# Four head chunks instead of five, an earlier start on TensorE, and equal shares of M's small reads

## The chip, the cores and the metric

The kernel runs on 1 core of one Trainium2 chip. The metric is the device time of one execution in microseconds (us), as the median of several runs. The span in a profile is from the first to the last instruction and lies 1.7 to 2.0 us below that time (in two runs 2.6 and 2.8). All runs quoted are of the state "fast". Ratios are the mean time of one kernel's fast runs over that of the other's fast runs of the same rounds, so not quite the ratio of the medians quoted beside them.

## The reference, cut to what matters

A three-layer cross network on x (1024 x 64 x 16, f32). For every layer: all products x[b,f,e] * h[b,g,e], then a contraction of the 64 x 64 (f, g) pairs with a weight matrix.

```python
x0 = h = x
for i in range(3):
    z = jnp.einsum('bfe,bge->bfge', x0, h).reshape(B, f0 * fh, e)
    y = jnp.einsum('oc,bce->boe', Ws[i], z) + bs[i][None, :, None]
    x_i, h = (y[:, :half], y[:, half:]) if i < 2 else (y, y)
    xs.append(x_i)
return jnp.sum(jnp.concatenate(xs, axis=1), axis=2) @ fc_w.T + fc_b
```

The last layer is only summed, so the kernel folds W2 and the final weights into W1 beforehand: the result is a matrix M, made on the chip. M has to be written to memory and read back with a skew and transposed, to become half of the weights `w_all`.

## The kernel before: what the change and the argument touch

The batch is cut into 32 chunks of 32 samples (512 columns). For each chunk VectorE makes four product tiles z (`product`), TensorE contracts them with `w_all`. Weights of the first layer (columns 0 to 63 of `w_all`) are there early; columns 64 to 127 need M. So a few "head" chunks are run with the first half alone while M is made and moved, and their second half later. Two of them, `KEPT`, keep their z tiles; the others' products are made again.

```python
HEAD = [4, 5, 6, 0, 1]; KEPT = HEAD[-2:]; FIRST = 8   # chunks from FIRST on run in groups of four
# (cut) head: chunks c0, c1; m_sb = M from w1s and v2t on TensorE; M written to md (HBM)
head(c2)                                      # products, first half, keep_h1 (ACT)
for half in range(2):                         # two large reads of M
    (nc.sync, nc.scalar)[half].dma_start(out=ms[halves[half], 0]..., in_=skewed(...))
for i in range(NI):                           # eight small reads, 256-byte rows
    for half in range(2):
        queue = nc.scalar if half and i < 2 else nc.sync
        queue.dma_start(out=ms[halves[half], 1]..., in_=skewed(...))
# (cut) dg and w_sq are read from md too
head(c3)
new_acc(c4, H2)                               # the fifth head chunk covers M's way
for j in range(NJ - 1):
    product(c4, j); half_contract(c4, 0, j)
nc.vector.tensor_tensor(w_all[:, 0:NT, 64:128], ms[:, 0], ms[:, 1], ALU.add)   # M is there
# (cut)
load_chunk(2); w1x = ...; nc.sync.dma_start(out=w1x, in_=wx1)
# (cut) second half of the kept chunks; then the main loop over chunks 2 to 31:
for s, c in enumerate(order):
    ahead = order[s + 2]                      # VectorE works two chunks ahead
    load_chunk(ahead); last_tile(ahead); [product(ahead, j) for j in range(NJ)]
    # contract c; per pair of chunks a tile y = bd x (PSUM, 2 buffers), combined on VectorE by x_v0x
```

`nc.sync` is the SP queue and `nc.scalar` the ACT queue. In the traces an engine's instructions and the DMAs that it gives out come in program order: after the change ACT gives out its five reads of M from 43.67 us on, and the square that the program puts behind them starts at 51.23.

## Time and profile before

| | before |
|---|---|
| time, median (6 runs) | 501.0 us (500.82 to 501.46) |
| span of the profile | 499.2 us |
| TensorE busy / VectorE busy | 483.8 us (97%) / 381.8 us (76%) |
| first matmul | 8.44 us |
| M added (start of that VectorE row) | 51.81 us |
| TensorE idle while M is on its way (from 40.5 us on) | none |

TensorE's row is the one to read: it is full from 40.5 us to the end of the last chunk, so a change gains by removing matmuls or by starting that full stretch sooner, and loses by opening a gap in it. The lines behind this stand in the prediction.

### The profile page before, as it was taken

What the parts mean: (1) busy time and instruction counts of PE and PEld (TensorE: products, weight loads), DVE (VectorE), ACT (ScalarE), POOL (GpSimd) and SP (SyncE); (2) the same over time, 40 slices, a digit from 0 to 9 for tenths busy, and PEclk for the clock granted to TensorE, in tenths of its full rate; (3) what the DMA queues carried; (4) which work ended last, traced back from release to release, by engine and by line L of the source; (5) the groups of instructions that cost most, each with busy time, mean ns of one, the idle gap of its engine ahead of it and who ended that gap; (6) DMA issues with size and microseconds to landing.
All of it is one profiled execution on the core that took longest, in us unless ns stands there. A gap on an engine that the chain in (4) does not pass through costs nothing.

```text
span 499.2 us, 4338 instructions
## 1 busy us (share of the span) xinstructions
PE 483.8 (97%) x1814; PEld 222.6 (45%) x1814; DVE 381.8 (76%) x233; ACT 92.5 (19%) x159; POOL 1.4 (0%) x14
## 2 busy tenths in 40 slices
PE   3899999999999999999999999999999999999996
PEld 1455654456444344443444434443444434444432
DVE  4999699988999889898777686776877777770302
ACT  1243033122111121312011121111111121010001
POOL 1000000000000000000000000000000000000000
PEclk9999999999999999999999999999999999999999
DMA  8997895353454443446144442333444430000000
GB/s 327 425 419 226 338 421 208 116 230 129 181 235 175 170 174 162 177 175 256 66 169 169 168 168 113 118 136 138 168 169 168 167 131 39 0 0 0 2 0 0
DMA packets 14787, 82.80 MB, mean 166 GB/s; under 512 B 3788, under 2 KB 4460, under 8 KB 5232
## 3 DMA queue, kind: packets, MB, share of 16 engines
q1 hardware_dynamic: 13644, 81.24, 41.5%
q10 hardware_dynamic: 1124, 1.29, 0.9%
q8 instruction: 14, 0.23, 0.2%
q14 instruction: 5, 0.04, 0.0%
HBM read 80.88 MB, written 1.64 MB: 165 GB/s over the span
## 4 chain that ended last, share of the span: by engine, by line
PE 91%; DMA 5%; ACT 1%; ACTq 0%; SPq 0%; DVE 0%; issue 0%
PE acc L198 75%; PE acc L237 11%; DMA w1s<-in_w1h 4%; PE acc L219 2%; DMA xb<-in_xrb 1%; PE acc L211 1%; PE y L267 1%; PE acc L205 1%; PE pm L336 0%; PE po L489 0%; ACT zl L175 0%; ACT zl L181 0%; ACT m_sb L341 0%; ACT xx L190 0%; ACTq L360 0%
## 5 line engine op out<-in xcount | busy, mean ns | idle before, releaser
L198 PE MATMUL acc<-z,w_all 128*128 128x512 f32 x864 | 374.1, 593 | 0.0
L166 DVE TENSOR_TENSOR z<-xa,xb 128x2048 f32<-128x2048 f32 (+1 forms) x141 | 314.9, 2270 | 49.9 <-PE acc L198 39.7
L198 PEld LDWEIGHTS acc<-z,w_all 128*128 128x128 f32 x864 | 163.3, 190 | 208.3 <-issue 207.8
L237 PE MATMUL acc<-z,w_all 128*64 128x256 f32 x640 | 74.7, 389 | 10.4 <-DVE w_all L282 8.4
L171 ACT ACTIVATE z<-xa 32x512 f32<-32x512 f32 x35 | 21.9, 625 | 323.5 <-DVE z L166 320.7
L263 DVE SCALAR_TENSOR_TENSOR uu<-acc,vs,q 64x512 f32<-64x512 f32 x27 | 20.2, 750 | 62.4 <-ACT q L262 62.3
L237 PEld LDWEIGHTS acc<-z,w_all 128*64 128x64 f32 x640 | 45.8, 140 | 39.1 <-DVE w_all L282 9.9
L274 DVE TENSOR_REDUCE acc<-uu 128x64 f32<-128x1024 f32 (+2 forms) x18 | 20.2, 1125 | 0.3
L190 ACT COPY xx<-xa 64x512 f32<-64x512 f32 x32 | 19.6, 613 | 0.4
L262 ACT COPY q<-acc 64x512 f32<-64x512 f32 x27 | 15.7, 580 | 19.3 <-PE y L224 12.9
L186 ACT ACTIVATE sq<-xa 32x512 f32<-32x512 f32 x24 | 15.1, 628 | 0.6
L270 DVE SCALAR_TENSOR_TENSOR uu<-y,cx,xx 128x512 f32<-128x512 f32 x16 | 11.4, 745 | 0.3
L224 PE MATMUL y<-xx,bd 64*64 64x512 f32 x48 | 11.6, 602 | 0.0
L219 PE MATMUL acc<-xx,v1w 64*64 64x512 f32 x48 | 11.6, 602 | 0.0
L211 PE MATMUL acc<-sq,w_sq 32*128 32x512 f32 x48 | 6.8, 640 | 0.0
L175 ACT ACTIVATE zl<-xa 64x512 f32<-64x512 f32 x11 | 6.8, 623 | 0.1
L219 PEld LDWEIGHTS acc<-xx,v1w 64*64 64x64 f32 x48 | 2.8, 132 | 7.9 <-issue 7.9
L237 PE MATMUL acc<-zl,w_all 64*64 64x256 f32 (+1 forms) x40 | 6.1, 393 | 0.0
L243 ACT ACTIVATE hb<-acc,vs 128x256 f32<-128x256 f32 x5 | 2.4, 474 | 20.0 <-PE acc L237 20.0
L495 ACT ACTIVATE res<-po,cst 2x480 f32<-2x480 f32 (+1 forms) x2 | 0.9, 464 | 24.0 <-PE po L489 24.0
L181 ACT COPY zl<-xa 64x512 f32<-64x512 f32 x8 | 4.9, 616 | 0.1
L256 DVE TENSOR_TENSOR uu<-acc,hb 64x256 f32<-64x256 f32 x10 | 4.2, 421 | 0.2
(52 smaller groups left out, 52.0 us busy)
## 6 DMA issues: line engine op xcount, KB each, us to landing
xa<-in_xra SPq DMA_DIRECT2D x34, 1024.0 KB, 4.8
xb<-in_xrb SPq DMA_DIRECT2D x34, 1024.0 KB, 7.0
w<-in_w2t SPq DMA_DIRECT2D x2, 1024.0 KB, 13.5
xa<-in_xra SPq DMA_DIRECT2D x2, 512.0 KB, 4.1
w1s<-in_w1h SPq DMA_DIRECT2D x1, 1024.0 KB, 20.3
w1x<-in_wx SPq DMA_DIRECT2D x1, 1024.0 KB, 8.7
w0x<-in_wx SPq DMA_DIRECT2D x1, 1024.0 KB, 10.3
xb<-in_xrb SPq DMA_DIRECT2D x1, 768.0 KB, 7.0
```

Of the source, the lines that this page charges most:

```text
L166: nc.vector.tensor_tensor(zs[c, j][:, i : i + n, :], xas[c][:, i : i + n, :], xbs[c][j].unsqueeze(1).to_broadcast([128, n, N]), ALU.mult,)
L171: nc.scalar.activation(zs[c, j][SQ, 0, :], xas[c][SQ, 0, :], AF.Square)
L186: nc.scalar.activation(zls[c // 4][at : at + 32], xas[c][0:32, 0, :], AF.Square)
L190: nc.scalar.copy(xxs[c // 2][to], xas[c][to, 0, :])
L198: nc.tensor.matmul(accs[c], w_all[:, t, w_cols(c)], zs[c, j][:, i, :], start=(t == 0 and (c < FIRST or c % 4 < 2)), stop=(t == NT - 1 and ...
L211: nc.tensor.matmul(accs[c], w_sq[at, w_cols(c)], zls[first // 4][at], start=(r >= 2), stop=(r < 2), tile_position=(32 * r, 0),)
L219: nc.tensor.matmul(accs[c][q], v1w[rows], xxs[k][rows], start=False, stop=(c % 4 < 2), skip_group_check=True,)
L224: nc.tensor.matmul(ys[k][rows], bd[rows, rows], xxs[k][rows], start=True, stop=True)
L237: nc.tensor.matmul(accs[c][halves[n]], w_all[rows, t, cols], z[rows, n * H2 : (n + 1) * H2], start=(t == 0), stop=(t == NT),)
L262: nc.scalar.copy(q[h], accs[c][64 - h.start : 128 - h.start])
L263: nc.vector.scalar_tensor_tensor(uu, accs[c][h], bh1[h], q[h], ALU.add, ALU.mult)
L274: nc.vector.tensor_reduce(acc[rows, parts, k, :], uus[k][rows, parts].rearrange("p k (b e) -> p k b e", e=E), AX.X, ALU.add,)
```

## The change

Its intent: one head chunk fewer and all other 28 chunks in shared groups (less work on TensorE), matmuls on zeros to warm the TensorE clock before data arrive, smaller first transfers, and the small reads of M shared equally by the two queues, since M has less cover now.

```diff
-HEAD = [4, 5, 6, 0, 1]
+HEAD = [2, 3, 0, 1]
-FIRST = 8
+FIRST = 4
+    pw = ps.tile([128, 128], F32, tag="y", name="pw")
+    for k in range(12):
+        nc.tensor.matmul(pw, bd, bd, start=True, stop=True)
-    load_xa(c0, slice(0, 2))
+    load_xa(c0, slice(0, 1))
     nc.sync.dma_start(out=xb0[:, 0, :], in_=xh)
+    nc.sync.dma_start(out=w0t[:, 0, :], in_=wh)
+    load_xa(c0, slice(1, 2))
     load_xa(c0, slice(2, 4))
-    nc.sync.dma_start(out=w0t[:, 0, :], in_=wh)
-    for j in range(NJ):
-        product(c0, j, 2 if j == 0 else 1)
+    product(c0, 0, 0, 1)
+    h1_weights(0)
+    product(c0, 0, 1, 2)
+    product(c0, 0, 2, 4)
+    for j in range(1, NJ):
+        product(c0, j)
-    load_chunk(c4)
-            queue = nc.scalar if half and i < 2 else nc.sync
+            queue = (nc.sync, nc.scalar)[half]
-    new_acc(c4, H2)      # (cut) the fifth head chunk, both parts
-    load_chunk(2)
+    load_chunk(FIRST)    # right behind M's reads on SP, as before
-    order = list(range(2, NCH))
+    order = [4, 5, 6, 7, 2, 3] + list(range(8, NCH))
# (cut) the loop's cases for chunks outside the groups; y0's combination stays after step 1's products
```

More of the change, by code (lines that the diff above doesn't have):

```diff
@@ L113, in cin_kernel @@
     nc.gpsimd.memset(bd, 0.0)
-    xas, xbs, zls, xxs = {}, {}, {}, {}
+    pw = ps.tile([128, 128], F32, tag="y", name="pw")
+    for k in range(12):
+        nc.tensor.matmul(pw, bd, bd, start=True, stop=True)
+    xas, xbs, zls, xxs, sqs = {}, {}, {}, {}, {}
     def load_xa(c, at=slice(0, NI)):
@@ L133, in load_chunk @@
         xbs[c] = [xb[:, j, :] for j in range(NJ)]
-    c0, c1, c2, c3, c4 = HEAD
+    c0, c1, c2, c3 = HEAD
     xb0 = z_tile("xb0")
@@ L160, in new_acc, with product @@
         accs[c] = ps.tile([128, n], F32, tag="acc", name=f"acc_{c}", bufs=4)
-    def product(c, j, pieces=1):
-        zs[c, j] = z_tile(f"z_{c}_{j}")
-        n = NI // pieces
-        for i in range(0, NI, n):
-            nc.vector.tensor_tensor(
-                zs[c, j][:, i : i + n, :], xas[c][:, i : i + n, :],
-                xbs[c][j].unsqueeze(1).to_broadcast([128, n, N]), ALU.mult,
-            )
+    def product(c, j, first=0, last=NI):
+        if first == 0:
+            zs[c, j] = z_tile(f"z_{c}_{j}")
+        at = slice(first, last)
+        nc.vector.tensor_tensor(
+            zs[c, j][:, at, :], xas[c][:, at, :],
+            xbs[c][j].unsqueeze(1).to_broadcast([128, last - first, N]), ALU.mult,
+        )
         if j == NJ - 1:
@@ L183, in last_tile @@
             if c % 4 == 0:
-                zls[c // 4] = xp.tile([128, N], F32, tag="zl", name=f"sq_{c}", bufs=4)
+                sqs[c // 4] = xp.tile([128, N], F32, tag="zl", name=f"sq_{c}", bufs=4)
             at = 32 * (c % 4)
-            nc.scalar.activation(zls[c // 4][at : at + 32], xas[c][0:32, 0, :], AF.Square)
+            nc.scalar.activation(sqs[c // 4][at : at + 32], xas[c][0:32, 0, :], AF.Square)
         if c % 2 == 0:
@@ L199, in contract @@
                 accs[c], w_all[:, t, w_cols(c)], zs[c, j][:, i, :],
-                start=(t == 0 and (c < FIRST or c % 4 < 2)),
-                stop=(t == NT - 1 and c >= FIRST and c % 4 >= 2),
-            )
-    def contract_last(c):
-        nc.tensor.matmul(accs[c], w_all[:, NT, 0:128], zls[c], start=False, stop=True)
+                start=(t == 0 and c % 4 < 2), stop=(t == NT - 1 and c % 4 >= 2),
+            )
     def contract_shared(first):
@@ L211, in contract_shared @@
             nc.tensor.matmul(
-                accs[c], w_sq[at, w_cols(c)], zls[first // 4][at], start=(r >= 2), stop=(r < 2),
+                accs[c], w_sq[at, w_cols(c)], sqs[first // 4][at], start=(r >= 2), stop=(r < 2),
                 tile_position=(32 * r, 0),
@@ L259, in factors @@
             return
-        h = halves[c % 2 if c >= FIRST else 0]
+        h = halves[c % 2]
         q = sp.tile([128, N], F32, tag="q", name=f"q_{c}")
@@ L408, in cin_kernel @@
     head(c3)
-    new_acc(c4, H2)
-    for j in range(NJ - 1):
-        product(c4, j)
-        half_contract(c4, 0, j)
     nc.vector.tensor_tensor(w_all[:, 0:NT, 64:128], ms[:, 0], ms[:, 1], ALU.add)
@@ L417, in cin_kernel @@
     nc.vector.tensor_copy(w_all[0:32, NT, 64:128], w_sq[0:32, 64:128])
-    product(c4, NJ - 1)
-    load_chunk(2)
+    load_chunk(FIRST)
     w1x = flat_tile("w1x")
     nc.sync.dma_start(out=w1x, in_=wx1)
-    new_acc(c3, H2)
-    for j in range(NJ):
-        half_contract(c3, 1, j)
-    for j in range(NJ - 1, NJ + 1):
-        half_contract(c4, 0, j)
-    keep_h1(c4)
-    new_acc(c4, H2)
-    for j in range(NJ):
-        half_contract(c4, 1, j)
+    for c in KEPT:
+        new_acc(c, H2)
+        for j in range(NJ):
+            half_contract(c, 1, j)
     def weigh(w, fc, out):
@@ L437, in weigh @@
         nc.vector.tensor_reduce(out, w, AX.X, ALU.add)
-    last_tile(2)
+    last_tile(FIRST)
     for j in range(NJ):
-        product(2, j)
+        product(FIRST, j)
     v1h = const_tile("v1h", [128, 32])
@@ L452, in cin_kernel @@
         nc.scalar.copy(w_sq[:, to], w0ds)
-    load_chunk(3)
+    load_chunk(FIRST + 1)
     w0x = flat_tile("w0x")
@@ L470, in cin_kernel @@
     nc.scalar.activation(cst, pc, AF.Identity, bias=fcb, scale=float(E))
-    last_tile(3)
+    last_tile(FIRST + 1)
     for j in range(NJ):
-        product(3, j)
+        product(FIRST + 1, j)
     v0h = const_tile("v0h", [128, 32])
@@ L496, in finish @@
         nc.scalar.dma_start(out=outs[:, pairs, :], in_=res[:, pairs, :])
-    order = list(range(2, NCH))
+    order = [4, 5, 6, 7, 2, 3] + list(range(8, NCH))
     first, last = slice(0, NP - 1), slice(NP - 1, NP)
     for s, c in enumerate(order):
-        k, shared = c // 2, c >= FIRST
+        k, head = c // 2, c in HEAD
         if s + 2 < len(order):
@@ L508, in cin_kernel @@
                 product(ahead, j)
-        if not shared or c % 4 < 2:
-            new_acc(c, H2 if c in HEAD else N)
+        if head or c % 4 < 2:
+            new_acc(c, H2 if head else N)
         for j in range(NJ):
@@ L517, in cin_kernel @@
                     v0x(0)
-                if c % 2 and not shared:
+                if head and c % 2:
                     v0x(k)
@@ L522, in cin_kernel @@
                     pool(first, 0)
-            if c in HEAD:
+            if head:
                 half_contract(c, 1, j)
@@ L526, in cin_kernel @@
                 contract(c, j)
-        if c in HEAD:
+        if head:
             half_contract(c, 1, NJ)
-        elif not shared:
-            contract_last(c)
         elif c % 4 == 1:
@@ L540, in cin_kernel @@
                 factors(n)
-        elif not shared or c % 4 in (0, 3):
+        elif head or c % 4 in (0, 3):
             factors(order[s - 1])
+            if order[s - 1] % 2:
+                sums(order[s - 1] // 2)
         elif c % 4 == 2:
@@ L547, in cin_kernel @@
             x_v0x(k)
+            sums(k - 1)
         if s == 1:
@@ L550, in cin_kernel @@
             sums(0)
-        if c % 2 and not shared:
+        if head and c % 2:
             x_v0x(k)
-        elif s and c % 2 == 0:
-            sums(k - 1)
     sums(NP - 1, parts=slice(1, 2))
```

## The prediction

> **What bounds the kernel now.** I read the page first (engines, the chain that ended last), then that chain in order of time, then the time line of the first 53 us by engine, then the DMA queues in steps of 1 us.
>
> ```profile
> PE 483.8 (97%) x1814; PEld 222.6 (45%) x1814; DVE 381.8 (76%) x233; ACT 92.5 (19%) x159; POOL 1.4 (0%) x14
> PE 91%; DMA 5%; ACT 1%; ACTq 0%; SPq 0%; DVE 0%; issue 0%
> L198 PE MATMUL acc<-z,w_all 128*128 128x512 f32 x864 | 374.1, 593 | 0.0
> L237 PE MATMUL acc<-z,w_all 128*64 128x256 f32 x640 | 74.7, 389 | 10.4 <-DVE w_all L282 8.4
> ```
>
> TensorE is busy for 97% of the span and is 91% of the chain. The line that holds most of the work (L198) never waits. Only 15.4 us of the span are without a matmul, 8.4 of them before the first one. So an engine other than TensorE can only matter in the head. In the chain in order of time (start, length, what) I look for the price of a chunk:
>
> ```profile
> 135.39 0.86 PE y L267 x2
> 136.25 6.87 PE acc L198 x16
> 143.11 0.86 PE acc L205 x2
> 143.97 27.47 PE acc L198 x64
> 171.44 1.07 PE acc L211 x8
> ...
> 174.39 55.13 PE acc L198 x128
> 229.52 1.07 PE acc L211 x8
> ```
>
> A matmul has two records, so a chunk's 16 are 32 records: 27.47 / 2 = 13.74 us. From 40.50 us to the end of the last chunk there is no gap. A shared group of four runs from 174.39 to 232.47 (171.44 + 2.95 of shared work to 174.39, and the next one likewise): 58.08 us, 14.52 for a chunk. A chunk outside the groups costs 13.74 + 0.86 (L205) + half of a 0.86 product with bd (L267) = 15.03.
>
> The head is different. The time line of DVE and of PE up to 53 us, in the brackets the idle time and who ended it:
>
> ```profile
> 5.62 2.43 DVE L166 TENSOR_TENSOR z<-xa,xb 128x1024 f32<-128x1024 f32 x2 [5.62 <-DMA xb<-in_xh]
> 9.58 2.29 DVE L166 TENSOR_TENSOR z<-xa,xb 128x2048 f32<-128x2048 f32 x1 [1.19 <-DMA xb<-in_xrb]
> 17.60 33.16 DVE L166 TENSOR_TENSOR z<-xa,xb 128x2048 f32<-128x2048 f32 x15
> 8.44 8.30 PE L237 MATMUL acc<-z,w_all 128*64 128x256 f32 x48 [8.44 <-DVE w_all L282]
> 17.73 1.95 PE L237 MATMUL acc<-z,w_all 128*64 128x256 f32 x16 [0.99 <-DVE w_all L294]
> 40.50 1.95 PE L237 MATMUL acc<-z,w_all 128*64 128x256 f32 x16 [0.77 <-ACT z L171]
> ```
>
> The first chunk is paced by VectorE, which itself waits at 9.58 us for a load, then has no gap until 50.76. After 17.73 TensorE idles for little more than 1 us in all until 50.6.
>
> **What the Trainium skill says.** (1) "TensorE: Matmul & The Clock Gate", Part 1, The HAM clock gate: the array starts at half clock and goes to full after some 3.4 us of activity. The trace agrees, though its granted-clock column reads 1.00 throughout: weight loads of the first block follow each other in pairs every 0.43 us between 8.93 and 11.06, and from 13.17 on ten take 1.08 us, 0.22 a pair; that is 4.7 us after the first matmul. (2) "DMA: Bandwidth & Descriptors", Queues, rings and completion order: an engine takes turns between the queues packet by packet. The trace agrees: from 38 to 39 us queue 10 (ACT) moved 31 packets and queue 1 (SP) 32. It also shows what I didn't find there: with queue 1 backed up, the writes of M issued on ACT at 33.57 moved no packet until 37.6. (3) Same page, Why small descriptors are slow: in the trace, 48 to 49 us, 783 packets of nearly all 256 bytes made 207 GB/s, against some 420 in the loads.
>
> **The change part by part.**
>
> Part A, four head chunks and seven groups. Removed from TensorE: the fifth head chunk's first part, 64 records in 7.13 us and 0.58 for its last tile (64.56 to 65.14) = 7.7; its second part in the main loop, (128.32 - 104.95 - 1.06) / 3 = 7.4, as three such chunks and one product with bd stand between these times; chunks 2, 3 and 7 of before at 13.74 + 0.86 = 14.60 each, 43.8; two products with bd, 1.7. In all 60.6. Added: one more group of four, 58.1. Net -2.6 us (an estimate from these durations), and all of it lies on the chain. On VectorE, four products of 2.28 go from the head: its 33.16 us for 15 products are 2.21 each, so the last product of the fourth chunk ends at 17.6 + 12 x 2.21 = 44.1, well ahead of TensorE.
>
> Part B, the start. First transfers of 0.25 MB: 0.25 MB less lies ahead of the first product, 0.6 us at 420 GB/s, so VectorE starts near 5.0 rather than 5.62; with its first weights pulled forward, TensorE's first real matmul could come at 6 to 7 us rather than 8.44. But the second product still waits for the landing at 9.58: the bytes ahead of it are the same 2.25 MB. From there the same row of VectorE work ends at 17.6, and TensorE's fourth block still waits for it. I count 0 for this (at most 0.2).
>
> Part C, 12 matmuls on zeros. 128 columns at half clock are half of the 0.43 us that a record pair of 256 columns took, for each of two records: 0.43 us a matmul, about 5 us for 12, from the end of bd's memset at 2.27 to about 7. They warm the clock before real work. What it saves is 16 records of 0.11 more each, 1.8 us, but in a stretch that VectorE paces (0.96, 0.5 and 0.99 us of idle follow each block anyway). Again 0 at the end.
>
> Part D, M's way through memory, which has to be covered by less work:
>
> ```profile
> 43.08 0.47 ACT L243 ACTIVATE hb<-acc,vs 128x256 f32<-128x256 f32 x1 [2.63 <-PE acc L237]
> 43.91 0.66 ACTq L393 DMA_DIRECT2D ms<-md  x1
> 44.60 1.54 ACTq L400 DMA_DIRECT2D ms<-md  x2
> 43.88 0.65 SPq L393 DMA_DIRECT2D ms<-md  x1
> 44.58 5.32 SPq L400 DMA_DIRECT2D ms<-md  x6
> 51.37 0.40 SPq L121 DMA_DIRECT2D xa<-in_xra  x1
> 51.81 1.23 DVE L415 TENSOR_TENSOR w_all<-ms 128x1024 f32<-128x1024 f32 x1 [1.04 <-DMA dg<-md]
> ```
>
> Before, M is added at 51.81 and ready by 53.5, while TensorE has the fifth chunk's 48 records to do. Now TensorE needs M right after the fourth chunk: 50.6 us, perhaps 0.6 earlier if ACT is freed sooner by quicker issues. What speeds M up: the fifth chunk's load (2 MB, 4.9 us at 422 GB/s) no longer stands ahead of the writes, so they land near 40.5 instead of 43.88. SP starts reading then; its one large, four small, dg and w_sq reads take some 4.6 us to issue, to about 45. What holds it back: ACT issues the other half, now five transfers, and its queue stands behind hb of the third chunk, 43.08 + 0.47, which hangs on TensorE and doesn't move much. Five issues of 0.66 to 0.77 end at about 47; the last starts near 46.4 and lands 3 to 5 us later (the small reads took 2.8 to 5.2 from issue to landing): 49.5 to 51.5. And from 45 SP puts 2 MB of chunk 4, w1x and another chunk into the queues. A small read is 64 KB in rows of 256 bytes, 16 packets an engine; taking turns with 8 KB packets (0.31 us each at 26 GB/s an engine), one such read can grow from 0.6 to 5 us. I take M landed at 51, the addition 1.25 us: TensorE starts on the kept chunks at 52.3 instead of 50.4, a new wait of 1.9 us.
>
> Sum: span 499.2 - 2.6 (A) - 0.2 (B, C, ACT) + 1.9 (D) = 498.3; the measured time is 500.94 - 499.2 = 1.74 above the span, so **500.0 us**. The parts nearly cancel.
>
> **The rivals.** (1) M in time. The author moved the reads to equal halves, which speaks for tuning on just this; the issue of eight small reads then takes four steps, not six. Then D is 0.2 to 0 and the time is 497.5 to 498. (2) M late by much: the last one or two reads on ACT fall behind or between chunk 4's load, as M's writes on ACT did from 33.57 to 37.6 in the kernel before. Each 1 MB put ahead is 2.5 us; two of them and taking turns make M land at 56 to 59, TensorE idle for 6 to 9 us and cold again after it (another 1.8). Then 505 to 509. For it speaks that ACT's issue can't start before 43.5; against it that the load of chunk 4 is issued about when ACT's last read is, not long before. (3) The warm start does shorten the head: if the first chunk were paced by TensorE, 2 us could go, 498 or less. The 0.99 us wait at 17.73 for w_all L294 speaks against it. (4) VectorE becomes the bound in the two short head chunks (2 and 3) of the main loop: 7.5 us of TensorE each against 8.9 of products. It runs two chunks ahead, and three such chunks in a row made no gap before, so I give it nothing.
>
> **Range and chances.** The floor is A and the start alone: 497.3. Late M has a longer tail: 505.5 holds most of rival 2. A gain of over 2% would need 10 us, and the removed work is 2.6: chance 0.02. A loss of over 2% needs M at 62 us: 0.05. Within 2%: 0.93.
>
> **What would show it right or wrong.** Right: the second product of the first chunk still starts near 9.6; the first chunk's last block on TensorE near 17.7; a gap of 0 to 4 us on TensorE ahead of the first kept chunk, ended by the addition of M or its copies; from there to the end 446 us with no gap; groups of 58.1. Part A is wrong if groups are longer or a gap stands in the main loop; B and C if the fourth block on TensorE comes a microsecond or more earlier; D if M is added before 49 or after 55. The prediction as a whole fails if M's reads are caught in the loads (rival 2) or if the head shrinks by several microseconds.

## The result, and the profile after

| | before | after |
|---|---|---|
| time, median | 501.0 us | **517.58 us** (516.75 to 517.84, 6 runs) |
| ratio | | 1.0326 (95%: 1.0313 to 1.034) |
| span | 499.2 | 515.4 |
| first real matmul | 8.44 | 7.34 |
| fourth block of the first chunk on TensorE | 17.73 | 17.71 |
| first half of the fourth chunk done on TensorE | 50.6 | 55.7 |
| M added | 51.81 | 64.68 |
| kept chunks start on TensorE | no gap | 66.05 |
| mean granted clock | 0.999 | 0.983 |

The change is 3.3% slower. In the profile after, the time line of ACT, SP, VectorE and TensorE around M (start, length, what, and in brackets the idle time before and who ended it):

```profile
43.67 0.64 ACTq L398 DMA_DIRECT2D ms<-md  x1
46.36 4.83 ACTq L405 DMA_DIRECT2D ms<-md  x4
51.23 0.62 ACT L177 ACTIVATE z<-xa 32x512 f32<-32x512 f32 x1 [7.30 <-issue]
...
48.11 0.37 SPq L126 DMA_DIRECT2D xa<-in_xra  x1
48.97 0.36 SPq L137 DMA_DIRECT2D xb<-in_xrb  x1
49.87 0.33 SPq L420 DMA_DIRECT2D w1x<-in_wx  x1
...
64.68 1.23 DVE L415 TENSOR_TENSOR w_all<-ms 128x1024 f32<-128x1024 f32 x1 [19.15 <-DMA ms<-md]
...
51.91 3.26 PE L239 MATMUL acc<-z,w_all 128*64 128x256 f32 x16 [3.17 <-ACT z L177]
66.05 14.21 PE L239 MATMUL acc<-z,w_all 128*64 128x256 f32 x104 [10.30 <-DVE w_all L415]
```

Three things are to be seen. ACT's four small reads are given out over 4.83 us, the last at 50.51, while SP has gone on to the loads of chunk 4, w1x and chunk 5 from 48.11. The last read lands only just before the addition. And ACT's square for the fourth chunk (L177) stands behind those issues, which keeps TensorE waiting 3.17 us already before M.

In the chain that ended last, in order of time, the wait carries its length:

```profile
43.89 5.26 DMA ms<-md
49.15 0.02 issue
49.17 0.58 ACTq L405
...
49.79 0.68 ACTq L405
50.47 0.04 issue
50.51 13.88 DMA ms<-md
...
64.68 1.24 DVE w_all L415
65.92 0.14 issue
66.05 16.80 PE acc L239 x128
```

The last read takes 13.88 us to land, for 64 KB; the two before it, given out at 49.17 and 49.79, are under way with it. What the DMA engines did meanwhile, in the view of the DMA queues for 55 to 56 us (packets, MB, share of 16 engines):

```profile
q1 hardware_dynamic: 53, 0.40, 95.6%
q10 hardware_dynamic: 53, 0.01, 6.0%
```

Packets alternate one for one: 53 of SP's loads of up to 8 KB each, 53 of M's of 256 bytes. M's reads get 6% of the engines' time. This goes on from 53 to 62 us; at 63 to 64, with the loads done, the same queue moves 236 packets in one microsecond. Before that, from 49.5 to 52.9 us, queue 10 moves no packet at all, though reads were given out on it at 49.17, 49.79 and 50.51; why is not shown.

And the windows (busy time of PE, PEld, DVE, ACT and POOL with counts, then granted clock, DMA share, GB/s):

```profile
50.00:55.00 5.00, 3.09 (x16) 1.65 (x16) 0.00 (x0) 0.62 (x1) 0.00 (x0) 0.66 0.99 381
60.00:65.00 5.00, 0.00 (x0) 0.00 (x0) 0.32 (x1) 0.00 (x0) 0.00 (x0) 0.50 0.67 242
65.00:70.00 5.00, 3.95 (x20) 2.57 (x22) 4.93 (x5) 0.00 (x0) 0.00 (x0) 0.50 0.00 0
```

The clock is at half when the kept chunks start.

**The sum.** Up to the start of the kept chunks, TensorE loses 66.05 - 50.6 = 15.5 us: 0.4 before the fourth chunk, 3.2 waiting for ACT's square, 1.3 on that block at half clock (3.26 against 1.95), 10.3 waiting for M, and 0.3 of rounding and gaps between rows. The kept chunks take 16.80 instead of 14.0 us, as they do in a warm run (e1 below), another 2.8. Part A gives back about 2. That makes 16.3; the spans differ by 16.2.

Why ACT gives its reads out so late stands in the waits that the program built from the kernel carries. The DMAs of both queues together take eight completion semaphores in turn (DMAHW0 to 7), and one that takes a semaphore again waits until the transfer that used it last has landed:

```
ACT 27 L245 Activation hb<-acc_325,vs   [waits PE]
ACT 28 L398 DMACopy ms<-md 64x4x256     [waits DMAHW4,5,3,6,2,1]
ACT 29 L405 DMACopy ms<-md 64x4x64      [waits DMAHW7]
ACT 30 L405 DMACopy ms<-md 64x4x64      [waits DMAHW1]
ACT 31 L405 DMACopy ms<-md 64x4x64      [waits DMAHW2]
ACT 32 L405 DMACopy ms<-md 64x4x64      [waits DMAHW3]
ACT 33 L177 Activation z_3_391<-xa_193  [waits DVE]
```

Each small read on ACT waits for an earlier transfer to land, and the square stands behind all of them. In the same program the last users of these four semaphores are SP's own reads of M: its large one (DMAHW7) and its second, third and fourth small ones (DMAHW1 to 3). The times agree. SP's large read was given out at 42.54 and landed 3.8 us later, and ACT's first small read goes out at 46.36; SP's second small read, the 5.26 us at the head of the chain above, landed at 49.15, and ACT's second goes out at 49.17. In the kernel before, ACT's two small reads carry no such wait. This is read from the program and the trace; no run tests it by itself.

### The profile page after: what moved, and what is told of

The parts are those of the page before. It is cut to its first block, busy times and chain, and to the rows that moved or that the text cites. A ratio compares the mean times of both kernels' runs of the same rounds, so it can differ in the third digit from the quotient of the medians.

```text
span 515.4 us, 4187 instructions
## 1 busy us (share of the span) xinstructions
PE 489.2 (95%) x1748; PEld 224.8 (44%) x1748; DVE 373.9 (73%) x229; ACT 89.9 (17%) x154; POOL 1.4 (0%) x14
## 4 chain that ended last, share of the span: by engine, by line
PE 87%; DMA 10%; SPq 1%; DVE 1%; ACT 0%; issue 0%; ACTq 0%; DVEq 0%
PE acc L204 75%; PE acc L239 6%; DMA w1s<-in_w1h 4%; DMA ms<-md 4%; PE acc L221 2%; PE acc L213 1%; DMA md<-m_sb 1%; DMA xb<-in_xrb 1%; PE pm L341 0%; PE po L485 0%; PE y L269 0%; ACTq L405 0%; SPq L126 0%; DVE w_all L415 0%; ACT m_sb L346 0%
## 5 line engine op out<-in xcount | busy, mean ns | idle before, releaser
L204 PE MATMUL acc<-z,w_all 128*128 128x512 f32 x896 | 387.6, 593 | 0.0
L172 DVE TENSOR_TENSOR z<-xa,xb 128x2048 f32<-128x2048 f32 (+1 forms) x138 | 307.0, 2255 | 55.6 <-PE acc L204 47.7
L204 PEld LDWEIGHTS acc<-z,w_all 128*128 128x128 f32 x896 | 169.3, 190 | 216.3 <-issue 216.3
L177 ACT ACTIVATE z<-xa 32x512 f32<-32x512 f32 x34 | 21.3, 625 | 351.1 <-DVE z L172 343.7
L239 PE MATMUL acc<-z,w_all 128*64 128x256 f32 x512 | 62.8, 401 | 18.6 <-DVE w_all L415 10.3
L239 PEld LDWEIGHTS acc<-z,w_all 128*64 128x64 f32 x512 | 38.5, 144 | 43.1 <-issue 14.7
L264 ACT COPY q<-acc 64x512 f32<-64x512 f32 x28 | 16.2, 580 | 19.4 <-PE y L226 12.9
L192 ACT ACTIVATE sq<-xa 32x512 f32<-32x512 f32 x28 | 17.6, 627 | 0.6
L226 PE MATMUL y<-xx,bd 64*64 64x512 f32 x56 | 13.8, 604 | 0.0
L272 DVE SCALAR_TENSOR_TENSOR uu<-y,cx,xx 128x512 f32<-128x512 f32 x16 | 11.4, 746 | 0.3
L118 PE MATMUL pw<-bd 128*128 128x128 f32 x24 | 5.1, 405 | 2.3 <-POOL bd L113 2.3
L118 PEld LDWEIGHTS pw<-bd 128*128 128x128 f32 x24 | 4.9, 315 | 2.3 <-POOL bd L113 2.3
L213 PEld LDWEIGHTS acc<-sq,w_sq 32*128 32x128 f32 x56 | 2.2, 182 | 5.3 <-issue 5.3
```

Source lines behind the costliest of these rows:

```text
L172: nc.vector.tensor_tensor(zs[c, j][:, at, :], xas[c][:, at, :], xbs[c][j].unsqueeze(1).to_broadcast([128, last - first, N]), ALU.mult,)
L177: nc.scalar.activation(zs[c, j][SQ, 0, :], xas[c][SQ, 0, :], AF.Square)
L192: nc.scalar.activation(sqs[c // 4][at : at + 32], xas[c][0:32, 0, :], AF.Square)
L204: nc.tensor.matmul(accs[c], w_all[:, t, w_cols(c)], zs[c, j][:, i, :], start=(t == 0 and c % 4 < 2), stop=(t == NT - 1 and c % 4 >= 2),)
L213: nc.tensor.matmul(accs[c], w_sq[at, w_cols(c)], sqs[first // 4][at], start=(r >= 2), stop=(r < 2), tile_position=(32 * r, 0),)
L226: nc.tensor.matmul(ys[k][rows], bd[rows, rows], xxs[k][rows], start=True, stop=True)
```

## The experiments

Eleven kernels ran; all gave the right result. Three jobs on three chips; the kernel before was at 501.17, 501.36 and 501.37 us there, and at 501.0 in the runs of the result, so times of different jobs can be compared to some 0.4 us.

**e1: the small reads shared as before, all else as changed.**

```diff
-            queue = (nc.sync, nc.scalar)[half]
+            queue = nc.scalar if half and i < 2 else nc.sync
```

> The changed kernel, with the small reads of M shared between the queues as before (six on SP, two on ACT). Theory 1 (ACT's late reads are caught in SP's loads of chunk 4): SP now gives out its six before its loads, M is added near 52 us instead of 64.7, TensorE starts on the kept chunks near 53, stays warm or nearly so, span near 499 to 501, time 500 to 503. Theory 2 (four head chunks cover too little, whatever the queues): M is added at 57 or later, and the time stays above 506.

Measured: 510.53 us, ratio 1.0189. M is added at 51.38 and the kept chunks run from 52.76 with a warm clock, as theory 1 said to within 0.7 us. But the time is 9 us above the middle of the 500 to 503 us that it made of this. The time line of e1, VectorE and TensorE:

```profile
57.72 8.90 DVE L172 TENSOR_TENSOR z<-xa,xb 128x2048 f32<-128x2048 f32 x4 [4.68 <-DMA xb<-in_xrb]
...
96.97 8.90 DVE L172 TENSOR_TENSOR z<-xa,xb 128x2048 f32<-128x2048 f32 x4
105.89 0.75 DVE L272 SCALAR_TENSOR_TENSOR uu<-y,cx,xx 128x512 f32<-128x512 f32 x1
...
106.70 1.97 PE L226 MATMUL y<-xx,bd 64*64 64x512 f32 x4 [6.66 <-DVE uu L272]
```

The first shared group needs two y tiles in PSUM, of which y0 still holds one. Only VectorE's combination (L272) frees it, and that stands behind chunk 7's products. VectorE started the chain when chunk 4 had landed, at 57.72, and needs 48.9 us to that point. In the changed kernel this wait was there too, but only 0.4 us of it showed (L272 ended at 115.2, TensorE's second y pair began at 115.23), because M had held TensorE for longer. So the wait for M had hidden a second one almost as late.

**e2: equal halves kept, SP's loads held back until M is added.** The load of chunk 4 has to wait for a memset that VectorE does after M's additions; SP's later loads stand behind it.

```diff
+    xas[FIRST] = xp.tile([128, NI, N], F32, tag="xa", ...)
+    nc.vector.memset(xas[FIRST][:, 0, 0:1], 0.0)     # after the additions on VectorE
     load_chunk(FIRST)                                 # (does not make its own tile now)
```

> The changed kernel with its equal halves kept, but SP's loads of chunk 4, w1x and chunk 5 held back until M is added (a memset of one column of chunk 4's tile by VectorE after the additions, which the load has to wait for). Theory 1 (caught in the loads): the last reads on ACT, given out at 50.5, land in 3 to 5 us instead of 13.9, M is added near 55, TensorE starts near 56.5; time 504 to 507, a gain of 10 to 13. Rival (the reads on ACT are slow of themselves, by issue and lanes): they still land after 60 and the time stays above 513.

Measured: 514.58 us, ratio 1.0273. M is added at 52.86 instead of 64.68, with the longest of its transfers 4.7 us from issue to landing instead of 13.9: for M, theory 1 holds. The time gains only 3 us, since chunk 4 lands late (its products start at 61.75), and TensorE waits 6.7 us for L272 again. The expectation for the time failed for the same reason as in e1.

**e3: the kernel before with the equal halves alone.**

```diff
-            queue = nc.scalar if half and i < 2 else nc.sync
+            queue = (nc.sync, nc.scalar)[half]
```

> The kernel before, five head chunks, with nothing changed but the equal halves of the small reads. Theory 1: M is added at 58 to 65 instead of 51.8, TensorE runs out of work near 56 to 57 (48 records of the fifth chunk) and waits; time 505 to 512. Theory 2 (only the shorter head costs): the fifth chunk covers it, time 501, the same within 0.3%.

Measured: 503.56 us, ratio 1.0052 (1.0037 to 1.0067). Between the theories. M is added at 52.35, only half a microsecond later than before: here SP's own dg and w_sq reads had to wait for completion semaphores too (w_sq went out at 50.99), so its loads began at 51.69, after ACT's last read. What costs the 2.4 us is the other half of the mechanism: ACT's four small reads take 5.67 us to give out, and the square behind them comes at 50.28:

```profile
50.95 1.95 PE L237 MATMUL acc<-z,w_all 128*64 128x256 f32 x16 [2.62 <-ACT z L171]
```

So equal halves cost 2.4 us even with five head chunks, and the loads catch M's reads only where SP gets to them early enough (from 48.11 in the changed kernel, from 51.69 here).

**e4: the kernel before with the new start alone** (12 matmuls on zeros, 0.25 MB transfers, weights pulled forward; the lines of the diff above).

> The kernel before with the start of the changed one alone: 12 matmuls on zeros, first transfers of 0.25 MB, first weights pulled forward. My account of parts B and C: the first real matmul comes near 7.3 us instead of 8.44, the fourth block still near 17.7, time 501.0 within 0.5 us. Rival: the warm start shortens the head by 1 to 2 us, time 499 to 500.

Measured: 500.94 us against 501.17, ratio 1.0003 (0.9988 to 1.0017). No effect on the median, as parts B and C said. But the profiled run, at 502.07 the slowest of four, shows something that neither account had:

```profile
13.08 8.25 PE L242 MATMUL acc<-z,w_all 128*64 128x256 f32 x48 [2.36 <-DVE w_all L287]
21.26 0.65 PE L242 MATMUL acc<-zl,w_all 64*64 64x256 f32 x4
```

and its windows (TensorE busy with the count of records, granted clock, DMA share, GB/s):

```profile
12.00:14.00 2.00, 0.92 (x6) 0.52 1.00 422
14.00:16.00 2.00, 2.00 (x12) 0.50 1.05 442
```

The 48 records of the last three blocks run on to 21.3; in the kernel before the same chunk's last tile came at 19.61. The granted clock is 0.52 to 0.50 from 12 to 18 us. The zeros had warmed the clock early (the first four records take 0.65 us here, 1.12 in e10 without zeros), then TensorE was busy for only 2.3 of the 5 us from 7 to 12, and the clock fell again just when the dense work came.

**e5: e1 with y0's combination ahead of chunk 7's products.**

```diff
 # step s == 1 of the main loop
-    [product(ahead, j) for j in range(NJ)]        # before contract(5)
     v0x(0)                                        # TensorE, inside contract(5)
+    x_v0x(0); sums(0)
+    [product(ahead, j) for j in range(NJ)]
-    x_v0x(0); sums(0)                             # after contract(5)
```

> e1 (M's small reads shared as before) with one more edit: the combination of y0 and its sum go ahead of chunk 7's products on VectorE, so that y0's PSUM buffer is free when the first shared group wants it. Theory A (in e1 TensorE lost its gain waiting 6.7 us for that buffer, as VectorE reached it only after chunk 7's products): the wait goes, with 1 to 2 us of cold clock after it; span near 499 to 500, time 500.5 to 502. Rival (VectorE is behind anyway, another wait takes its place at once): over 506.

Measured: 501.05 us, ratio 0.9996 (0.9979 to 1.0012). The time line, VectorE and TensorE:

```profile
51.16 1.22 DVE L415 TENSOR_TENSOR w_all<-ms 128x1024 f32<-128x1024 f32 x1 [5.83 <-DMA ms<-md]
...
52.54 14.03 PE L239 MATMUL acc<-z,w_all 128*64 128x256 f32 x128
```

The wait for y is gone from the list of waits, M is added at 51.16, the kept chunks start at 52.54, and nothing waits in the first group. Theory A holds. ACT's two small reads still go out slowly, from 46.41 to 49.35, but here SP's loads start behind them, at 49.69. So the changed kernel with its reads shared as before and one reordering is as fast as the kernel before.

**e6: the changed kernel with that same edit alone.**

> The changed kernel with the same edit on y0 and nothing else. There M's additions at 64.7 hold TensorE, and the wait for y was 0.4 us: time 516.5 to 518, the same as the changed kernel. If it gains over 2 us, the buffer was a bound in the changed kernel too.

Measured: 517.77 us, ratio 1.0329. No gain, as expected: with M added at 65.39, y is no bound. e5 and e6 differ in the queue line alone, and that is 16.7 us.

**e11: e6 with SP's loads held back as in e2.**

> Both: SP's loads held back until M is added (as in e2), and y0's combination ahead of chunk 7's products (as in e5 and e6). Equal halves and four head chunks stay. If the loads that catch M's reads are the main loss of the changed kernel and the wait for y's buffer only hid that in e2, this gains 10 us or more over e6: M added near 53, kept chunks from 54, the first group held a little by VectorE, which starts late (61.8) because the loads start late; time 503 to 507. If the loads were not the cause, it stays near e2's 514.

Measured: 504.78 us, ratio 1.0075. 13.0 us below e6 by the hold alone, with equal halves kept. The time line:

```profile
52.34 1.22 DVE L415 TENSOR_TENSOR w_all<-ms 128x1024 f32<-128x1024 f32 x1 [6.59 <-DMA ms<-md]
...
51.13 3.00 PE L239 MATMUL acc<-z,w_all 128*64 128x256 f32 x16 [2.17 <-ACT z L177]
...
55.12 14.09 PE L239 MATMUL acc<-z,w_all 128*64 128x256 f32 x128
```

That settles the main cause: M's reads were caught in SP's loads. What is left to e5 (3.7 us) is ACT's late square (2.17 here, 1.18 in e5), the cold clock after it (3.00 against 1.95 on that block, and the last tile at 1.12 instead of 0.65), and a first group held 1.3 us longer, by ACT's squares, which wait for VectorE's products, because the loads start late (VectorE begins on chunk 4 at 61.44 here, at 57.55 in e5).

**e7 and e12: e6 with 40 and with 54 matmuls on zeros in the gap before the kept chunks.**

```diff
+    pg = ps.tile([128, 128], F32, tag="y", name="pg")
+    for k in range(40):                               # 54 in e12
+        nc.tensor.matmul(pg, bd, bd, start=True, stop=True)
     for c in KEPT:
```

> e6 with 40 more matmuls on zeros on TensorE between the fourth chunk's first part and the kept chunks, some 8.6 us at full clock, so that the gap of 10.3 us is filled and the clock stays up. The cold clock cost the kept chunks 16.80 - 14.3 = 2.5 us, and a little more: time 2.5 to 3.5 us below e6. Rival: the clock was not what made the kept chunks slow: same as e6, or longer by what the zeros overrun.

Measured: 516.82 us (515.48 to 518.35), ratio 1.031. Not a test: the zeros ended 3.25 us before M came, the clock fell to 0.59 at 68 to 70 us, and the kept chunks took 15.72 us.

> e7 with 54 matmuls on zeros in the gap instead of 40: in e7 they ended 3.25 us before M, and the clock fell to half again. 54 are 12.4 us, up to within 0.5 us of M. If the cold clock is what makes the kept chunks 15.5 us long in e6, they take 14.0 now and the time is 1 to 2 us below e6's 517.8, 515.5 to 517; if not, they stay at 15.5 and the time too.

Measured: 516.41 us (515.0 to 518.37), ratio 1.03. The kept chunks, of e6 and then of e12:

```profile
66.76 15.52 PE L239 MATMUL acc<-z,w_all 128*64 128x256 f32 x128 [11.30 <-DVE w_all L415]
```

```profile
56.41 12.32 PE L425 MATMUL pg<-bd 128*128 128x128 f32 x108
68.66 14.03 PE L239 MATMUL acc<-z,w_all 128*64 128x256 f32 x128
```

With no idle time ahead they run at full clock: 14.03 us. So the clock is what makes them slow. The time hardly shows it, as in this run M was ready at 66.5 and the zeros ran on to 68.7; the medians of e6 and e12 differ by 1.4 us with runs that overlap.

**e9: a version to beat both.** Four head chunks, all small reads on SP, and the order of work set right.

```diff
-            queue = (nc.sync, nc.scalar)[half]
+            queue = nc.sync                       # ACT keeps one large read
-    load_chunk(c2); (load of w1s)
+    (load of w1s); load_chunk(c2)
# M's matmuls before the third block of c1; v2's regrouping (pt) after its first block
# last_tile of the kept chunks (ACT) after the third chunk's square and M's read
-    load_chunk(FIRST); (load of w1x)              # and product(FIRST) before weigh(w1x)
+    (load of w1x); load_chunk(FIRST)              # and weigh(w1x) before product(FIRST)
# step 0: loads and last_tile of chunks 6 and 7, factors of the kept chunks, then product(6)
# step 1: y0's combination, then product(7), as in e5
```

> An attempt at a version that beats both: e5's idea with M sooner and VectorE's work in the order of need. All small reads of M on SP and one large one on ACT; w1's load ahead of the third chunk's; M's products two blocks earlier on TensorE; the squares of the third chunk ahead of the kept chunks' on ACT; w1x loaded and weighed ahead of chunk 4's products; the kept chunks' factors and y0's combination ahead of chunks 6 and 7. M should be added near 50 to 51, the kept chunks start near 51 to 52, and nothing wait in the first group: span near 497, time 498 to 500. If VectorE or the order of its work still binds, a wait in the first group and 501 or more.

Measured: **498.91 us** (498.65 to 500.27), ratio 0.9957 (0.9943 to 0.9972): 0.43% faster than the kernel before. M is added at 50.92, and TensorE waits 0.67 us for it:

```profile
52.29 14.03 PE L239 MATMUL acc<-z,w_all 128*64 128x256 f32 x128 [0.67 <-DVE w_all L414]
```

That profile is of the slowest run (500.27), in which the clock fell at the start as in e4; the other three lie within 0.32 us.

**e10: e9 without the 12 matmuls on zeros.**

> e9 without the 12 matmuls on zeros at the start. In the profiles of e2, e4, e7 and e9 the granted clock fell to half at 12 to 18 us, after the zeros had warmed it early and TensorE then idled for 2 us; in the kernel before, which starts cold at 8.44, it never did. So without zeros the first chunk should end near 20.2 in every run: time 498.4 to 499.0 and a spread under 0.5 us, where e9 had 498.65 to 500.27. Rival: the zeros help (earlier first blocks), 499.5 or more without them.

Measured: 499.7 us (499.49 to 500.5, 5 runs), ratio 0.9968 (0.9955 to 0.998). The first part of the expectation held (the profile has a granted clock of 1.00 throughout), the rest failed: the median is no better than e9's and the spread 1.0 us. Without the zeros the first blocks themselves run at the slow rate until about 16 us (12 records in the 2 us from 14, 22 from 18). So the zeros may help by up to a microsecond or cost one, by where the clock falls; the intervals of e9 and e10 overlap, and the net value stays open.

## Why the prediction was wrong, point by point

The prediction was 500.0 us with 497.3 to 505.5; measured 517.58. What failed is Part D, the wait for M: its mechanism was seen, its size was not, and that size is nearly the whole result.

**Part D: "a new wait of 1.9 us".** Measured 15.5 us to the start of the kept chunks and 2.8 us of cold clock in them. Four of its terms failed:

- "So they land near 40.5": M's writes landed at 42.3. SP's first read went out at 42.54, and SP was through with its seven reads at 47.7 instead of 45.
- "Five issues of 0.66 to 0.77 end at about 47; the last starts near 46.4". They ran from 43.67 to 51.19 and the last began at 50.51. I took the issue times from a kernel in which ACT gave out three reads, none of which had to wait for another read of M. With five, the four small ones wait for the landing of SP's reads, eight completion semaphores being used in turn by both queues. The start at 43.5 was right.
- "lands 3 to 5 us later". It landed 13.9 us later. The alternation of packets was in the prediction, seen in the trace and worked out (0.6 to 5 us for a small read), but its sum made little use of it. By its own times the loads (from 45) were out before ACT's last read (46.4), and yet it took M as landed at 51, 4.6 us after that. Being late by 4 us put three of the four small reads behind the start of 5 MB of loads (48.11), not one; at 5 us each that is up to 15 us (an estimate by the prediction's own arithmetic, until the loads are through). e11 against e6 shows it: 13.0 us by holding the loads alone.
- What stands behind the issues on ACT was not looked at. The square comes behind the issues in ACT's program, so ACT idled 7.3 us before its square and TensorE 3.17. e3 shows this part by itself, 2.4 us.

**Rival 2** named the right mechanism, with M landing at 56 to 59 and 505 to 509 us. It was still too mild: M was added at 64.68, and the range cut it short: 505.5 does not hold "most of rival 2" but only the low end of its own 505 to 509. The argument against it, that chunk 4's load goes out "about when ACT's last read is, not long before", was the error: 48.11 against 50.51.

**Part A** was right in kind. e5 runs 446.6 us from the start of the kept chunks to the end of the span, where the prediction had 446 and the kernel before took 448.6 from 50.6. So the removed work is worth 2.0 rather than 2.6 us. It is spent again: in e5 the kept chunks start at 52.5 instead of 50.6.

**Parts B and C** held. The second product of the first chunk started at 9.55, the fourth block at 17.71 (17.73 before), and e4 is at 1.0003; only the first real matmul, at 7.34, came later than the 6 to 7 expected. Rival 3 is out. That the zeros can make the head slower, by a clock that falls once more, was missed.

**Rival 4, "I give it nothing"**, failed, though not where it looked. In the two short chunks nothing waits. But from chunk 4's landing VectorE has 48.9 us of work up to the release of y0, and with M in time TensorE arrives there 6.7 us early (e1, e2). In the changed kernel this was hidden. In the kernel before, the third y tile was wanted at 115.83 and y0 had been freed at 109.6, so nothing showed; the regrouping asks for it sooner in VectorE's order.

**The chances** (0.05 for slower) treated the late M as a tail. The profile of before held both facts that should have made it wide: writes issued on ACT that moved no packet for 4 us behind SP's queue, and packets going one for one.

**What stays open:** the value of the zeros at the start within a microsecond either way, and why queue 10 moved no packet from 49.5 to 52.9 us, before the taking of turns began.

## What to carry to other kernels

When a change takes cover away from a round trip through memory, follow every transfer of that trip from issue to landing: which engine's queue it stands in and behind what, which earlier landing its issue waits for, and which bulk loads go out before it. Small reads that gate work belong ahead of bulk loads. Shared equally over two queues here, they were passed by the bulk (16.7 us between e5 and e6) and blocked the second engine's compute (2.4 us in e3). One queue that gives out both in that order avoids this; e9 does so, but with other edits, so its worth by itself is not shown. And after removing the longest wait, look for the next chain that ends almost as late: here it was a PSUM buffer, and freeing it earlier by one reordering turned 510.5 us into 501.

## What the Trainium skill lacked or had wrong

- "DMA: Bandwidth & Descriptors", Queues, rings and completion order: its taking turns by packets is confirmed (53 to 53 in 1 us), but it gives a packet as typically 9 to 17 descriptors. In these traces rows of 256 bytes and of 8 KB were counted as packets of their own, so a 256-byte read got 6.0% of the engines against 95.6%. What this does to a small read beside a load is not said: 13.9 us to landing, against 2.8 to 5.5 for the small reads of the kernel before.
- Same page, Issuing engines are not separate DMA queues: it says that issuing from several engines saves only the sequencer's time. The runs show that it can cost: 16.7 us between e5 and e6, by the queue of two small reads.
- Same page: nothing was found there, for loads and stores within one core, on a second queue's transfers moving nothing while the first is backed up (0 packets of queue 10 from 33.57 to 37.6 in the kernel before, and from 49.5 to 52.9 after the change).
- "TensorE: Matmul & The Clock Gate", Why this matters for your kernels: no idle gaps over some 3 us, or the clock falls. In e7 it fell after 3.25 us. But in e4 it fell at the start with gaps of at most 2.4 us, after a stretch in which TensorE was busy 2.3 of 5 us (7 to 12), so this rule by the longest gap is not enough. (The page's passage on a second failure mode does tell of short, frequent idle times that make the clock swing; e4 is in line with it.)
- No page was found that has a completion semaphore's reuse as something that delays an issue: ACT's four small reads took 4.83 us to give out, SP's four 2.69.
